# The order of reads in a paged-attention kernel: queries before probabilities, and the second query weights one slot sooner

## The chip, the cores and the metric

The kernel runs on one core of a Trainium2 chip, in one launch. The metric is the time of the execution on the device in microseconds (us). Single executions of the same kernel differ: the three timed ones of the kernel before lie between 1224.23 and 1229.9 us.

## The reference: what is computed

Everything is float32. There are B = 8 sequences of S = 128 tokens with 512 channels. First each sequence gets a LoRA-like product with the adapter that its id selects, and then attention over a paged cache and over its own new keys and values:

```
x = x + einsum('bsi,boi->bso', x, weight[adapter_ids])          # 512 x 512 per sequence
q, k, v = x @ Wq.T, x @ Wk.T, x @ Wv.T                          # 32 query heads, 8 key heads, D = 128
q, k = rope(rmsnorm(q, q_norm_w), pos), rope(rmsnorm(k, k_norm_w), pos)
k_all = concat([k_cache[block_table], k]);  v_all = concat([v_cache[block_table], v])   # 512 + 128 keys
scores = q . k_all / sqrt(128), cache keys past cache_seqlens masked out
o = softmax(scores) . v_all                                     # 4 query heads share a key head
x = x + o @ Wo.T
```

## The kernel before, in words

**Groups and steps.** The 8 key heads are cut into G = 4 groups of 2, each with its 8 query heads. The main loop runs over 32 steps: step i is group g = i // 8 and sequence b = i % 8. The weights of a group are loaded once and serve its 8 steps; steps 7, 15 and 23 are the last of their groups and already project the first sequence of the next group.

**Slots.** A step has 8 slots, h = 0 to 7, one for each query head of the group; slot number 8 * i + h orders them all. Heads 0 to 3 are the first half (j = 0), heads 4 to 7 the second (j = 1). In a slot TensorE computes the scores sc of one head (line 977, 128 queries by 640 keys) from the turned queries qT and the turned keys kT; VectorE adds the mask and takes the row's extreme (line 987); ScalarE takes the exponential (line 1003); GpSimd multiplies by the reciprocal of the row's sum (line 1052). Between the scores TensorE does pieces of a list called main: projections pj_kv and pj_q for step i + 1, products of probabilities and values o for step i - 1, and the output projection out for step i - 2 or i - 1. All these pieces are issued at line 508. From step 6 on main holds, in this order, pj_kv and q0's pj_q of step i + 1, o of step i - 1 for the first half, q1's pj_q of step i + 1, o of step i - 1 for the second half, and out. In steps 1 to 5 o comes first and the adapter's product y is among them.

**Turning by way of DRAM.** Operands that TensorE needs turned (transposed) are turned in blocks of 32 by VectorE, written to DRAM, and read back in another order. There are four such streams, named by their tiles:

- probabilities of one half: tp is written to xp (send, line 837, 1280 KB), and xp is read to pT (receive, line 846, 1280 KB);
- queries of one half: tq to xq (send_q, line 757, 256 KB), xq to qT (line 764, 256 KB);
- keys of a step: tk to xk (line 739, 512 KB), xk to kT per key head (line 747, 256 KB);
- weights of the next group, in pieces of 128 rows: tw to xw (line 465, on ScalarE's queue), and xw to w_kv, w_q or w_o (receive_weights, line 473, 256 KB each, on ScalarE's queue). In the profile q0 and q1, the weights of the first and of the second four query heads, both show as w_q. Each has four pieces, n = 0 to 3, and a projection needs all four.

**Who issues what.** Writes and reads of probabilities, queries and keys are issued by SyncE (SP) in program order; reads of turned weights by ScalarE (ACT), between its computations; the gathers of cached keys and values kc and vc by GpSimd. A read waits for the landing of the write that it follows. The framework gives every transfer of SP and ACT one of eight semaphores, which are used again and again, and an issue also waits for the last transfer of its semaphore.

**When a read is issued.** A read of probabilities or queries isn't issued in the slot of its write but in a later one. The list to_read keeps it with its write's slot number; in each slot, after the exponential and the weight reads, those of earlier slots are issued in the order in which they were appended. send(u) appends in the slot after a half's fourth head; a query's send_q is called from the list later, run just after that, so that in a slot where both are appended the probabilities stand first. Reads of weights stand in a table by slot, made before the loop: read_at(slot, key). With B = 8, kv's four reads are in slots h = 2 to 5 of a group's seventh step (6, 14 and 22), q0's in slots 4 to 7 of it, and q1's in its slot 7 and in slots 0 to 2 of the next step. The tile of q1 has one buffer; its old weights are last used by the projection for the group's last sequence, in slot 4 of the seventh step.

Of the kernel before, what the change touches and what calls it, by code (L numbers as in the profile page):

```python
# [19 lines left out]
B = 8  # L20
# [32 lines left out]
def lora_then_paged_attention(  # L53
# [219 lines left out]
    def read_at(slot, key):  # L273
        reads_at.setdefault(slot, []).append(key)

    for g in range(1, G):
        before = 8 * B * (g - 1)
        for k, kind in enumerate(("kv", "q0", "q1")):
            for n in range(4):
                turn_when[before + 9 + 5 * (4 * k + n) // 2] = len(turns_of)  # L280
                turns_of.append((kind, g, n))
                read_at(before + 8 * (B - 2) + (2, 4, 7)[k] + n, (kind, g, n))
        for n, slot in enumerate((39, 42, 45, 62, 64, 66, 68, 70)):
            key = (f"o{n // 4}", g, n % 4)
            turn_when[before + slot] = len(turns_of)
            turns_of.append(key)
            read_at(8 * (B * g + 1) + n - n // 4 * 2, key)
# [440 lines left out]
    to_read = []  # L728
# [23 lines left out]
    def send_q(i, n):  # L752
        s = st[i]
        tq = work.tile([P, 4, 4, Q4], FP, tag=f"tq{n}", name=f"tq_{i}_{n}")
        nc.vector.transpose(tq, s.q[n].rearrange("p h (a d) -> p a h d", a=4))
        xq = xch.tile([4, P, 4, Q4], FP, tag=f"xq{n}", name=f"xq_{i}_{n}")
        nc.sync.dma_start(
            out=xq.rearrange("b (i a) h q -> (b i) (a h q)", a=4),
            in_=tq.rearrange("p a h q -> p (a h q)"),
        )  # L760

        def receive():
            s.qT[n] = work.tile([P, 4, 4, Q4], FP, tag=f"qT{n}", name=f"qT_{i}_{n}")
            nc.sync.dma_start(
                out=s.qT[n].rearrange("d b h q -> d b (h q)"),
                in_=xq.rearrange("b d h q -> d b (h q)"),
            )

        to_read.append((now[0], receive))

    now = [0]

# [69 lines left out]
    def receive(u):  # L842

        pl, tag = (lora, "raw") if u.j and u.i >= B - 3 else (pts, "pT")
        pT = pl.tile([P, 4, REP, QK], FP, tag=tag, name=f"pT_{u.i}_{u.j}")
        nc.sync.dma_start(
            out=pT.rearrange("p b r k -> p b (r k)"), in_=u.scr.rearrange("b p x -> p b x")
        )
        st[u.i].pT[u.j] = pT

    def run(queue):
        calls = list(queue)
        queue.clear()
        for f in calls:
            f()
# [80 lines left out]
    for i, (g, b) in enumerate(steps):  # L936
        s = st[i]
        main = []
        if i == 0:
            main += project(0, "q1")  # L940
        early = i >= B - 2
        if i and not early:
            main += values(i - 1, 0)
        if i < last:
            main += project(i + 1, "kv") + project(i + 1, "q0")
        if early:
            main += values(i - 1, 0)
        if i == last:
            main += output(i - 2)
        if g == 0 and b + 2 < B and i:  # L950
            main += lora_y(b + 2)
        if i and not early:
            main += values(i - 1, 1)
        if i < last:
            main += project(i + 1, "q1")
        if early and i < last:
            main += values(i - 1, 1)
        if i == 0:
            main += lora_y(2)
        if i == last:  # L960
            pieces = output(i - 1)
            main += pieces[:3] + values(i - 1, 1, True) + pieces[3:]
        elif i and i != last - 1:
            main += output(i - 1)
        unit = None
        for h in range(8):
            j, r = h // 4, h % 4
            if r == 0:
                unit = Unit()
                unit.i, unit.j, unit.p = i, j, {}  # L970
                unit.mn, unit.sm, unit.rc = (
                    small.tile([P, REP], FP, tag=t, name=f"{t}_{i}_{j}") for t in ("mn", "sm", "rc")
                )

            sc = ps_sc.tile([P, 1024], FP, tag="sc", name=f"sc_{i}_{h}")
            for lo, hi in ((0, L), (L, LA)):
                nc.tensor.matmul(  # L977
                    sc[:, lo:hi],
                    lhsT=s.qT[j][:, r, :, :].rearrange("d h q -> d (h q)"),
                    rhs=s.kT[j].rearrange("d a c i -> d (a c i)")[:, lo:hi],  # L980
                    start=True,
                    stop=True,
                )
            p = probs.tile([P, LA], FP, tag="p", name=f"p_{i}_{h}")
            unit.p[r] = p
            one = slice(r, r + 1)
            nc.vector.tensor_tensor_reduce(  # L987
                out=p,
                in0=sc[:, 0:LA],
                in1=masks[i % 2].rearrange("p a c i -> p (a c i)"),  # L990
                scale=1.0,
                scalar=3.0e38,
                op0=ALU.add,
                op1=ALU.min,
                accum_out=unit.mn[:, one],
            )
            now[0] = 8 * i + h
            run(pending)
            turns = turns_at.pop((i, h), [])
            for early, _, f in turns:  # L1000
                if early:
                    f()
            nc.scalar.activation(  # L1003
                p, p, AF.Exp, bias=unit.mn[:, one], scale=-1.0, accum_out=unit.sm[:, one]
            )
            if prev is not None:
                u, pr = prev
                if u.i < last or u.j == 0:
                    turn_p(u, pr)
                if pr == REP - 1:  # L1010
                    send(u)
                    to_read.append((8 * i + h, lambda u=u: receive(u)))
            run(later)
            run(to_write)
            if 8 * i + h in turn_when:
                to_write.append(send_weights(*turns_of[turn_when[8 * i + h]]))
            for key in reads_at.get(8 * i + h, []):
                receive_weights(*key)
            for _ in range(len(to_read)):
                when, f = to_read.pop(0)  # L1020
                if when < 8 * i + h:
                    f()
                else:
                    to_read.append((when, f))
            if h == 0 and i:
                receive_k(i, 1)
            if h == (1 if i else 3) and i < last:
                send_k(i + 1)
            if h == 4 and i < last:
                receive_k(i + 1, 0)  # L1030

            ahead = sum(c for k in range(h + 1, 8) for _, c, _ in turns_at.get((i, k), []))
            mine = sum(t[1] for t in turns)
            share = (sum(c for c, _ in main) + ahead + mine) / (8 - h) - mine
            took = 0.0
            while main and (h == 7 or took + main[0][0] / 2 <= share):
                cost, f = main.pop(0)
                f()
                took += cost
            for early, _, f in turns:  # L1040
                if not early:
                    f()
            if i == last and h > 4:
                turn_p_pe(*prev)
            nc.vector.reciprocal(unit.rc[:, one], unit.sm[:, one])  # L1045
            q = p
            if i == last and j == 1:

                unit.p[r] = probs.tile([P, LA], FP, tag="p", name=f"pk_{h}")
                p = p.rearrange("q (a c i) -> q a c i", a=4, c=NC)  # L1050
                q = unit.p[r].rearrange("q (c i a) -> q a c i", a=4, c=NC)
            nc.gpsimd.tensor_scalar(q, p, unit.rc[:, one], 1.0, ALU.mult, ALU.mult)  # L1052
            prev = (unit, r)

            if i < last:
                if i + 1 < last and h in ((3, 5) if i else (4, 5)):
                    c = 0 if h < 5 else 2
                    gather_k(i + 2, c)
                    gather_k(i + 2, c + 1)
                for c in {6: (0, 1), 7: (2, 3)}.get(h, ()) if i else (range(LC) if h == 7 else ()):  # L1060
                    gather_v(i + 1, c)
                if h == 6:
                    pending.append(lambda i=i: make_mask(i + 1))
            if g == 0 and h == 6 and b + 3 < B:
                load_x(b + 3)
                gather_lora(b + 3)
            if 8 * i + h - 1 in turn_when:
                load_next()
# [58 lines left out]
```

## Time and profile before

| what | value |
|---|---|
| median of three runs | 1227.44 us (1224.23 to 1229.9) |
| the profiled execution's own time | 1228.89 us |
| its span, first to last instruction | 1227.1 us |
| mean granted TensorE clock | 0.99 |
| TensorE (PE) busy | 1188.1 us, 97% |
| VectorE (DVE), GpSimd (POOL), ScalarE (ACT) busy | 729.9, 675.3 and 531.0 us |
| bytes moved by DMA | 328.26 MB, 267 GB/s over the span |

The page and the answers of the trace name an engine, a line and the tiles: `PE sc L977 <- DMA qT<-xq` is TensorE's work on the scores at line 977, which waited for the transfer from xq to qT. Matmuls overlap and their ends are modelled, so the start of one is the safer mark. A line of a timeline gives start and length in us, the engine, the line, the operation and the tiles, how many were merged (x), and in brackets the idle time before and who ended it. SPq and ACTq are the issuing of DMAs; the length there is that of the issue, not of the transfer. The time to landing comes from a query on the single transfer. Steps are told from each other by the first score matmul of each: step 6 starts at 289.96 us, step 7 at 330.18, step 15 at 612.07 and step 23 at 896.60.

### The profile page before, as it was taken

To read this page: it belongs to the slowest core of one execution; us is meant where nothing else is said; L and a number is where in the kernel's file an instruction comes from. 1 tells how busy PE (TensorE), PEld (TensorE's weight loads), DVE (VectorE), ACT (ScalarE), POOL (GpSimd) and SP (SyncE) were. 2 spreads that over 40 slices of the span, in tenths; PEclk is the share of its full clock that TensorE was granted. 3 is DMA by queue.
4 is the path that set the end of the run, shared out by engine and by line. 5 is a ranking of instruction groups with operands and counts; after the bars stand their busy time and mean duration, and the time that the engine had idled before them with its cause. 6 is when DMAs were issued, how large, how long until landed. Compare 5 with 4: busy or idle time off the path is not lost.

```text
span 1227.1 us, 12945 instructions
## 1 busy us (share of the span) xinstructions
PE 1188.1 (97%) x3408; PEld 579.5 (47%) x3408; DVE 729.9 (59%) x1670; ACT 531.0 (43%) x1649; POOL 675.3 (55%) x778
## 2 busy tenths in 40 slices
PE   5889999999899999999989999999989999999998
PEld 3554554454344444444434444444434444444445
DVE  4456666565466666666547666666556656655651
ACT  4454444444344444444434444444434444444442
POOL 5464546455555556556635556655555566555541
PEclk9989999999899999999989999999999999999999
DMA  8267798877878989888878998888898897777761
GB/s 298 87 233 246 257 310 276 282 252 264 266 253 282 334 293 323 279 297 275 294 244 278 311 353 285 286 296 283 275 297 264 281 306 244 263 232 256 260 226 60
DMA packets 187496, 328.26 MB, mean 267 GB/s; under 512 B 13440, under 2 KB 106496, under 8 KB 178336
## 3 DMA queue, kind: packets, MB, share of 16 engines
q1 hardware_dynamic: 124112, 239.23, 58.1%
q10 hardware_dynamic: 50096, 48.22, 12.1%
q0 software_dynamic: 13216, 39.99, 9.7%
q8 instruction: 27, 0.44, 0.1%
q14 instruction: 45, 0.37, 0.1%
HBM read 195.27 MB, written 132.12 MB: 267 GB/s over the span
## 4 chain that ended last, share of the span: by engine, by line
PE 91%; DMA 3%; POOL 2%; ACT 2%; issue 1%; DVE 1%; ACTq 0%
PE sc L977 22%; PE o L508 21%; PE pj_q L508 18%; PE out L508 17%; PE pj_kv L508 9%; PE y L508 2%; DMA qT<-xq 1%; PE lw L430 1%; DMA bt_i<-in_itok_Bx_dram 1%; DMA w_q<-xw_q 1%; DMA xq<-tq 1%; DMA w_o<-xw_o 1%; PE x L430 1%; PE kt L711 1%; ACT sq L595 0%
## 5 line engine op out<-in xcount | busy, mean ns | idle before, releaser
L987 DVE CUSTOM_DVE_ANT_0 p<-sc,mask 128x640 f32<-128x640 f32 x256 | 211.0, 824 | 425.0 <-PE sc L977 424.8
L1003 ACT ACTIVATE p<-p,mn 128x640 f32<-128x640 f32 x256 | 211.6, 827 | 346.8 <-DVE mn L987 337.2
L977 PE MATMUL sc<-kT,qT 128*128 128x512 f32 (+1 forms) x1024 | 320.9, 436 | 7.8 <-DMA qT<-xq 4.1
L1052 POOL TENSOR_SCALAR p<-p,rc 128x640 f32<-128x640 f32 x252 | 201.6, 800 | 211.8 <-DVE rc L1045 210.0
L977 PEld LDWEIGHTS sc<-kT,qT 128*128 128x128 f32 x1024 | 191.0, 191 | 235.5 <-issue 213.4
L508 PE MATMUL pj_q<-w_q,x1T 128*128 128x512 f32 x512 | 242.6, 605 | 8.5 <-DMA w_q<-xw_q 4.0
L508 PE MATMUL o<-pT,vc 128*128 128x512 f32 x512 | 237.4, 594 | 0.0
L508 PE MATMUL out<-w_o,oT 128*128 128x512 f32 (+1 forms) x528 | 235.1, 580 | 2.1 <-ACT oT L786 0.7
L819 DVE STREAM_TRANSPOSE tp<-p 128x640 f32<-128x640 f32 x252 | 211.0, 837 | 4.4 <-POOL p L1052 4.1
L559 POOL DMA_INDIRECT kc<-in_L_cond_k_cache_dram,key_ix x128 | 130.9, 1023 | 31.8 <-issue 30.2
L559 POOL DMA_INDIRECT vc<-in_L_cond_v_cache_dram,val_ix x128 | 128.2, 1002 | 31.2 <-issue 31.2
L508 PEld LDWEIGHTS pj_q<-w_q,x1T 128*128 128x128 f32 x512 | 94.1, 195 | 103.6 <-issue 100.5
L640 ACT ACTIVATE q<-q,rs 128x128 f32<-128x128 f32 x256 | 81.9, 391 | 139.1 <-POOL q L627 136.0
L508 PEld LDWEIGHTS out<-w_o,oT 128*128 128x128 f32 x528 | 95.7, 190 | 95.1 <-issue 91.5
L508 PEld LDWEIGHTS o<-pT,vc 128*128 128x128 f32 x512 | 92.2, 191 | 89.0 <-issue 81.8
L508 PE MATMUL pj_kv<-w_kv,x1T 128*128 128x512 f32 x256 | 118.7, 602 | 0.7 <-ACT x1T L432 0.7
L620 POOL TENSOR_TENSOR k<-sw 128x256 f32<-128x256 f32 x31 | 22.9, 740 | 159.8 <-PE kt L711 134.4
L627 POOL TENSOR_TENSOR q<-q,sw 128x512 f32<-128x512 f32 x61 | 77.2, 1265 | 48.6 <-DVE sw L611 48.6
L595 ACT ACTIVATE sq<-pj_q 128x128 f32<-128x128 f32 x256 | 70.7, 276 | 48.3 <-PE pj_q L508 40.3
L635 POOL TENSOR_TENSOR rs<-ss,mhalf 128x6 f32<-128x6 f32 x64 | 77.6, 1213 | 5.3
L508 PEld LDWEIGHTS pj_kv<-w_kv,x1T 128*128 128x128 f32 x256 | 46.8, 194 | 47.4 <-issue 45.7
L508 PE MATMUL o<-pT,vn 128*128 128x512 f32 x128 | 65.4, 593 | 0.0
(112 smaller groups left out, 866.3 us busy)
## 6 DMA issues: line engine op xcount, KB each, us to landing
xp<-tp SPq DMA_DIRECT2D x63, 1280.0 KB, 5.8
pT<-xp SPq DMA_DIRECT2D x63, 1280.0 KB, 6.8
xk<-tk SPq DMA_DIRECT2D x31, 512.0 KB, 7.7
kT<-xk SPq DMA_DIRECT2D x62, 256.0 KB, 6.5
xq<-tq SPq DMA_DIRECT2D x59, 256.0 KB, 4.3
qT<-xq SPq DMA_DIRECT2D x59, 256.0 KB, 6.1
st_q<-in_L_cond_Wq_dram ACTq DMA_DIRECT2D x24, 256.0 KB, 5.4
xw_q<-tw_q ACTq DMA_DIRECT2D x24, 256.0 KB, 4.0
```

The lines of the kernel that those rows point to most:

```text
L430: nc.tensor.transpose(t[:, j, :], blk, ident)
L508: nc.tensor.matmul(y[0], lhsT=lhsT, rhs=rhs, start=(k == 0), stop=(k == len(pieces) - 1))
L559: nc.gpsimd.indirect_dma_start(out=dst[:, c, :], out_offset=None, in_=src, in_offset=bass.IndirectOffsetOnAxis(ap=rows[:, g, at : at + 1], ...
L595: nc.scalar.activation(sq, t[:, h, :], AF.Square, scale=float(D) ** -0.5, accum_out=ss[:, h : h + 1])
L627: nc.gpsimd.tensor_tensor(dst, cw, sw[:, 0:heads, :], ALU.add)
L635: nc.gpsimd.tensor_tensor(rs[:, 0:width], ss[:, 0:width], mhalf[:, 0:width], ALU.pow)
L640: nc.scalar.activation(q, q, AF.Identity, scale=rs[:, h : h + 1])
L819: nc.vector.transpose(u.tp[:, :, r, :], u.p.pop(r).rearrange("q (a k) -> q a k", a=4))
L977: nc.tensor.matmul(sc[:, lo:hi], lhsT=s.qT[j][:, r, :, :].rearrange("d h q -> d (h q)"), rhs=s.kT[j].rearrange("d a c i -> d (a c i)")[:, ...
L987: nc.vector.tensor_tensor_reduce(out=p, in0=sc[:, 0:LA], in1=masks[i % 2].rearrange("p a c i -> p (a c i)"), scale=1.0, scalar=3.0e38, op0 ...
L1003: nc.scalar.activation(p, p, AF.Exp, bias=unit.mn[:, one], scale=-1.0, accum_out=unit.sm[:, one])
L1052: nc.gpsimd.tensor_scalar(q, p, unit.rc[:, one], 1.0, ALU.mult, ALU.mult)
```

## The change

Two things. An entry of to_read gets a rank, 0 for queries and 1 for probabilities, and the entries that are due in a slot are issued in the order of rank. And the four q1 reads of each group are put into the table one slot sooner: slots 6 and 7 of the group's seventh step and slots 0 and 1 of the next.

```diff
         for k, kind in enumerate(("kv", "q0", "q1")):
             for n in range(4):
                 turn_when[before + 9 + 5 * (4 * k + n) // 2] = len(turns_of)
                 turns_of.append((kind, g, n))
-                read_at(before + 8 * (B - 2) + (2, 4, 7)[k] + n, (kind, g, n))
+                read_at(before + 8 * (B - 2) + (2, 4, 6)[k] + n, (kind, g, n))
...
-        to_read.append((now[0], receive))
+        to_read.append((now[0], 0, receive))
...
                 if pr == REP - 1:
                     send(u)
-                    to_read.append((8 * i + h, lambda u=u: receive(u)))
+                    to_read.append((8 * i + h, 1, lambda u=u: receive(u)))
...
             for key in reads_at.get(8 * i + h, []):
                 receive_weights(*key)
-            for _ in range(len(to_read)):
-                when, f = to_read.pop(0)
-                if when < 8 * i + h:
-                    f()
-                else:
-                    to_read.append((when, f))
+            due = [r for r in to_read if r[0] < 8 * i + h]
+            to_read[:] = [r for r in to_read if r[0] == 8 * i + h]
+
+            for _, _, f in sorted(due, key=lambda r: r[1]):
+                f()
             if h == 0 and i:
                 receive_k(i, 1)
```

## The prediction

> **What bounds the kernel now.** I read the page's busy times first.
>
> ```profile
> PE 1188.1 (97%) x3408; PEld 579.5 (47%) x3408; DVE 729.9 (59%) x1670; ACT 531.0 (43%) x1649; POOL 675.3 (55%) x778
> ```
>
> TensorE is busy for 1188.1 of 1227.1 us and the next engine for 730. Only TensorE's 39 us of idle time, and whatever slows its clock, can be won by moving transfers. So the second view is the waits of TensorE alone: who released it, sum, times, longest.
>
> ```profile
> PE lw L430 <- DMA raw_lora<-in_L_cond_weight_dram: 7.7, 1, 7.7
> PE sc L977 <- DMA qT<-xq: 4.1, 1, 4.1
> PE pj_q L508 <- DMA w_q<-xw_q: 4.0, 1, 4.0
> PE pj_q L508 <- issue: 3.9, 1, 3.9
> ```
>
> The first is the start of the program. The other three are single waits of about 4 us. The timeline of TensorE puts them at 326.13-330.18, 627.82-631.78 and 912.35-916.23: the three changes of group, in steps 7, 15 and 23. The third has no named releaser, but the last read of w_q before it, issued at 907.88, took 8.2 us and landed at 916.04, so it is the same wait as the second.
>
> ```profile
> 626.80 1.02 PE L508 MATMUL o<-pT,vn 128*128 128x512 f32 x2
> 631.78 5.28 PE L508 MATMUL pj_q<-w_q,x1T 128*128 128x512 f32 x6 [3.96 <-DMA w_q<-xw_q]
> 636.90 1.24 PE L977 MATMUL sc<-kT,qT 128*128 128x512 f32 x4
> ```
>
> Six such matmuls take 2.74 us elsewhere and 5.28 after this wait. The stages say the same (columns: window, length, busy per engine, granted clock, DMA share, GB/s): the step of the wait, the undisturbed step after it, and the wait's own surroundings.
>
> ```profile
> 612.07:653.35 41.28, 37.32 (x95) 17.26 (x94) 21.19 (x50) 15.16 (x49) 20.27 (x24) 0.92 0.80 260
> 653.35:688.00 34.65, 34.65 (x96) 16.42 (x95) 24.02 (x53) 15.18 (x49) 20.46 (x24) 1.00 0.89 296
> 627.80:637.00 9.20, 5.24 (x8) 2.28 (x8) 1.82 (x7) 1.82 (x5) 2.85 (x4) 0.63 0.52 183
> ```
>
> The clock is 0.63 around the wait. A step without a wait repeats at 34.62 us from first score matmul to first score matmul, so a wait of 3.96 us costs 41.28 - 34.62 = 6.66.
>
> Two queue timelines show what is late. SP's at the first change of group:
>
> ```profile
> 311.54 0.33 SPq L837 DMA_DIRECT2D xp<-tp  x1
> 312.14 0.32 SPq L757 DMA_DIRECT2D xq<-tq  x1
> 318.56 0.37 SPq L846 DMA_DIRECT2D pT<-xp  x1
> 319.59 0.36 SPq L764 DMA_DIRECT2D qT<-xq  x1
> ```
>
> The 1280 KB read pT goes 1.0 us ahead of the 256 KB read qT. pT took 8.9 us and landed at 327.5; qT took 10.5 and landed at 330.05, 2.5 us behind it. ACT's at the second:
>
> ```profile
> 609.71 1.07 ACTq L473 DMA_DIRECT2D w_q<-xw_q  x2
> 614.33 0.37 ACTq L473 DMA_DIRECT2D w_q<-xw_q  x1
> 618.84 0.37 ACTq L473 DMA_DIRECT2D w_q<-xw_q  x1
> 623.36 0.43 ACTq L473 DMA_DIRECT2D w_q<-xw_q  x1
> ```
>
> The pair at 609.71 is the fourth q0 read and the first q1 read; the others are q1 reads two to four, one per slot. The last took 8.2 us, in company with a pT read, and landed at 631.54. The third took 6.0 and landed at 624.9.
>
> [...] waits of 3.9 to 4.05 us are followed by matmuls at up to double time (four score matmuls in 2.48 instead of 1.24 us at 330.18). The 0.65 us wait at 434.79 (step 9) made its step 35.51, a cost of 0.89: nearly its own length. [...]
>
> **The change part by part.** The built programs differ by no instruction on PE, DVE or POOL. On SP six pairs of reads swap: qT of step i goes ahead of pT of step i-1 for second halves in steps 2 to 6, and qT_7_0 goes ahead of pT_6_0. On ACT twelve reads (four q1 pieces, three times) move up one slot. Nothing is added.
>
> *Swap at step 7.* qT still waits for xq until 319.57, so its issue hardly moves; it loses pT in front. kT, the transfer before it, landed at 320.4. One 256 KB read takes about 2.5 us (330.05 - 327.5), so qT lands near 323-324, ahead of the 326.13 at which TensorE wants it. The wait of 4.05 goes. The slow stretch behind it goes too: the next score started 7.66 us later (330.18 to 337.84) where 4.52 is regular, so 3.14. Sum 7.19.
>
> *q1 reads at step 7.* The fourth was issued at 344.61, took 4.9 and landed at 349.5; TensorE waited until 349.71 (0.63, put down to ACT in the waits, though that was done). The interval was 5.38 against 4.51: 0.87. One slot earlier it is in time. Sum 0.87.
>
> *q1 reads at steps 15 and 23.* The fourth now goes out in the third's place: 618.84 and 903.37, landing (6.0 and 5.8) near 624.9 and 909.2, against 627.8 and 912.35. Spare: 2.9 and 3.2. Gains: 41.28 - 34.62 = 6.66, and 40.43 (896.60 to 937.03) - 34.62 = 5.81.
>
> *Swaps at steps 2 to 6.* No TensorE wait stands there, so they gain nothing here. pT is issued 1.2 us later (SP 136.29 and 137.09: the gap and one issue) and behind qT's bytes, and xk, queued next, moves as little. pT used to land at 145.4 and qT at 146.5; swapped, pT takes the later place. It is first used at 149.95: 3.4 spare. At step 6 it would land by 308, used at 311.44. Cost zero while that lasts; without it, each us missed costs at least one, six times.
>
> *What the first q1 read does.* It now leaves in the slot of q0's third read and stands ahead of q0's fourth in ACT's row. At step 15 q0's fourth landed at 616.9 and the next read 0.85 later, at 617.75; q0's projection starts at 617.66. Swapped places make it 0.1 + 0.24 (from landing to matmul, 631.54 to 631.78) = 0.3 late. At step 23 it would land at 901.85 for 902.19: just in time. At step 7 the projection moves to 338.92 - 7.19 = 331.7, and q0's fourth landed at 331.6; one read later would cost 0.9 + 0.2, but q0's third read (issued 319.83, landed 329.6) no longer stands wholly behind pT, so I take 0.4. With the 0.65 -> 0.89 ratio, together 0.9; bounds 0 and 3. On ACT it also stands ahead of the kT copy, which has 4 us (607.75 to 612.07). Each issue reuses one of eight semaphores and waits for that one's last transfer: at step 7 the first q1 read for a w_q read landed at 319.7, just before; ACT idles 9.1 us soon after.
>
> *Next late.* The pT read of the second half: at 623.41 (landed about 630.4), needed at 638.84 - 6.66 = 632.2, and no longer sharing with a q1 read. At step 23: 914.1 against 922.52 - 5.81 = 916.7. At step 7 SP holds xp until qT_7_1 is out at 331, so pT lands near 344 (xp 5.5, pT 7.0) against 346.2. Spare 1.8 to 2.6: no cost taken, 0 to 2 in the range.
>
> Sum: 7.19 + 0.87 + 6.66 + 5.81 - 0.9 = 19.6. The profiled execution took 1228.89 itself (span 1227.1), 1.45 above the median 1227.44: 1209.3 from it, 1207.8 from the median. I take **1208.5**.
>
> **Rivals.** (1) q0's fourth read becomes the late one: the tight margins above speak for it, the 0.85 us spacing of landings against more than 0.5. At 2 us each with some slow clock, three times 3: 1218. (2) The swap at step 7 does not help, because all transfers there share the engines and qT's 10.5 us is their load; for it, xq itself took 7.4; against it, qT landed right after pT. Then 7.2 less: 1216. (3) Slower: SP's queue. In steps 2 to 7 pT, xk and the next writes now stand behind qT's wait for xq. If that pushes pT past its 3.4 us at each of six places, [...] as priced above at 6.7. It decides once pT lands more than 7.4 us later than now; six such, 40, beat the 20 gained: 1248. The traced gap of 0.8 to 1.1 us between the two issues speaks against it. (4) The change does nothing that counts: another transfer, pT of the second half, stops TensorE at the same places within 6 us: 1222.
>
> **How the numbers follow.** About 0.5% (6.1 us) is what a measurement of this kernel can tell from no change. Chances: my forecast 0.67, (1) 0.14, (2) 0.11, (4) 0.05, (3) 0.03. Faster 0.92, same 0.05, slower 0.03. The range: forecast bounds run from 1228.89 - 20.5 - 1.45 - 1.9 = 1205 (no new cost, a little more where qT's spare of 0.4 to 0.6 us in steps 2 to 6 was used up in other executions) to 1213 (costs 3 and 2); taking in (2) makes it 1217.
>
> **What would show it.** Right: TensorE's waits lose all three 4 us rows; steps 15 and 23 last 34.6 to 35.2 us; the clock stays near 1.00 there; qT at step 7 lands within 5 us. Wrong in part: a wait at pj_q two slots before the old one (rival 1), at sc in step 7 (rival 2), at o from pT in steps 2 to 7 (rival 3) or right behind the removed waits (rival 4).

## The result, and the profile after

| kernel | median of its runs, us | lowest to highest |
|---|---|---|
| before | 1225.84 | 1222.3 to 1229.9 |
| after | 1210.08 | 1207.79 to 1210.96 |

The ratio of after to before is 0.9868, with a 95% interval of 0.9831 to 0.9904: faster by 1.3%. The forecast was 1208.5 (1205 to 1217). The profiled execution of after took 1210.85 us, with a span of 1209.1 and a mean clock of 0.997. It is 18.04 us shorter than the profiled one of before; the sum of the prediction was 19.6.

The page's busy times come first, as before. TensorE has lost 7.8 us of busy time, though it issues the same 3408 matmuls. That is slow clock that is gone (0.50 for 6.83, 6.83 and 3.41 us behind the three waits before): what the matmuls took there beyond their regular time comes to 3.3, 2.7 and 1.9 us.

```profile
PE 1180.3 (98%) x3408; PEld 577.2 (48%) x3408; DVE 729.9 (60%) x1670; ACT 531.0 (44%) x1649; POOL 675.2 (56%) x778
```

TensorE's waits (who released it, sum, times, longest):

```profile
PE lw L430 <- DMA raw_lora<-in_L_cond_weight_dram: 7.4, 1, 7.4
...
PE out L508 <- ACT p L1003: 2.0, 1, 2.0
...
PE out L508 <- DMA w_o<-xw_o: 1.3, 1, 1.3
...
PE pj_q L508 <- issue: 0.5, 1, 0.5
PE o L508 <- DMA pT<-xp: 0.2, 1, 0.2
```

The three rows of about 4 us are gone. What is left near their places is 0.5 us at pj_q in step 7, for q0's weights. Two rows at out are new in size: they stand in steps 9 and 17, the second step of the second and of the third group, and were 0.65 and 0.64 us before.

The timeline of TensorE at the second change of group. The six matmuls of q1 that took 5.28 us behind a wait take 2.74, with no wait in brackets:

```profile
621.35 2.74 PE L508 MATMUL pj_q<-w_q,x1T 128*128 128x512 f32 x6
623.92 1.24 PE L977 MATMUL sc<-kT,qT 128*128 128x512 f32 x4
```

The stages (window, length, busy per engine in the order PE, PEld, DVE, ACT, POOL, granted clock, DMA share, GB/s) say the same: step 15, the step behind it, and the 9.2 us around the former wait.

```profile
605.60:640.38 34.78, 34.78 (x96) 16.48 (x95) 21.18 (x50) 15.17 (x49) 20.25 (x24) 1.00 0.95 308
640.38:675.03 34.65, 34.65 (x96) 16.43 (x95) 24.02 (x53) 15.18 (x49) 20.45 (x24) 1.00 0.89 294
620.40:629.60 9.20, 9.20 (x28) 4.42 (x27) 4.37 (x11) 4.83 (x17) 5.71 (x8) 1.00 0.84 305
```

Step 15 is as long as its neighbour but for 0.13 us, and the clock, 0.63 around the wait before, is 1.00.

SP's queue at the first change of group, and ACT's at the second:

```profile
311.28 0.33 SPq L837 DMA_DIRECT2D xp<-tp  x1
311.87 0.32 SPq L757 DMA_DIRECT2D xq<-tq  x1
...
319.30 0.37 SPq L764 DMA_DIRECT2D qT<-xq  x1
319.76 0.48 SPq L846 DMA_DIRECT2D pT<-xp  x1
```

```profile
603.24 2.18 ACTq L473 DMA_DIRECT2D w_q<-xw_q  x2
...
607.85 0.37 ACTq L473 DMA_DIRECT2D w_q<-xw_q  x1
...
612.37 0.37 ACTq L473 DMA_DIRECT2D w_q<-xw_q  x1
```

On SP the two have changed places, and qT landed at 323.62, 4.3 us after its issue instead of 10.5. On ACT the last read of q1 now leaves at 612.37, ahead of the pT read at 617.87 instead of beside one, and landed at 619.30.

Step lengths, first score matmul to first score matmul, add up to the difference of the profiled executions. Step 6 is 36.00 and the others are 34.62 where none of these waits stands.

| place | before | after | measured | in the forecast's sum |
|---|---|---|---|---|
| steps 6 and 7 | 78.86 | 71.32 | -7.54 | -7.7 (7.19 + 0.87 - 0.4) |
| step 9 | 35.51 | 36.83 | +1.32 | 0 |
| step 15 | 41.28 | 34.78 | -6.50 | -6.4 (6.66 - 0.3) |
| step 17 | 35.50 | 36.13 | +0.63 | 0 |
| step 23 | 40.44 | 34.62 | -5.82 | -5.8 |
| sum | | | -17.91 | -19.6 (the 0.4 and 0.3 entered it as 0.9) |

Both kernels were profiled a second time (below). The same five places then took 231.22 us before and 212.83 after, so 18.4 less.

### The profile page after: what moved, and what is told of

Same layout as the page of the kernel before. It is cut to its first block, busy times and chain, and to the rows that moved or that the text cites. A ratio compares the mean times of both kernels' runs of the same rounds, so it can differ in the third digit from the quotient of the medians.

```text
span 1209.1 us, 12947 instructions
## 1 busy us (share of the span) xinstructions
PE 1180.3 (98%) x3408; PEld 577.2 (48%) x3408; DVE 729.9 (60%) x1670; ACT 531.0 (44%) x1649; POOL 675.2 (56%) x778
## 4 chain that ended last, share of the span: by engine, by line
PE 93%; DMA 2%; ACT 1%; POOL 1%; DVE 1%; issue 1%; ACTq 0%; SPq 0%
PE sc L977 22%; PE o L508 22%; PE out L508 18%; PE pj_q L508 18%; PE pj_kv L508 9%; PE y L508 2%; PE lw L430 1%; DMA bt_i<-in_itok_Bx_dram 1%; DMA w_o<-xw_o 1%; PE x L430 1%; PE kt L711 1%; DMA pT<-xp 0%; DMA xp<-tp 0%; ACT sq L595 0%; DVE p L987 0%
## 5 line engine op out<-in xcount | busy, mean ns | idle before, releaser
L508 PE MATMUL pj_q<-w_q,x1T 128*128 128x512 f32 x512 | 238.1, 595 | 0.5 <-issue 0.5
```

Of the source, the lines that this page charges most:

```text
L508: nc.tensor.matmul(y[0], lhsT=lhsT, rhs=rhs, start=(k == 0), stop=(k == len(pieces) - 1))
```

## The experiments

All ratios are to the kernel before, in runs on the same chip. Three sets were run: the first with before at 1228.19 us (median of 33 runs, 1220.08 to 1231.74), the second at 1227.08, the third at 1225.61. The ratios are those on record with their intervals; they need not be the quotient of two medians. A step's "extra" below is its length less the undisturbed length and less the wait itself.

### The swap alone

```diff
-read_at(before + 8 * (B - 2) + (2, 4, 6)[k] + n, (kind, g, n))    # after
+read_at(before + 8 * (B - 2) + (2, 4, 7)[k] + n, (kind, g, n))    # as in before
```

> The swap alone (queries read ahead of probabilities; q1's reads where they were). My theory: the wait at the first scores of step 7 goes (4.05 us and 3.14 of slow clock), q1's fourth read stays late in steps 7, 15 and 23, so about 7.2 us less than the kernel before, near 1219, steps 15 and 23 at 41.3 and 40.4 us. Rival (shared load, not order, made qT late): no more than 1 us less, near 1225, with a wait of 3 to 4 us at sc in step 7. On the output weights: if the wait at out in step 9 grew from 0.65 to 1.97 us because step 7 lost its stall, it is near 2 here in step 9 and near 0.65 in step 17; if it is chance, neither need hold.

Measured: 1224.65 us (1221.05 to 1231.63), ratio 0.9998 [0.9974, 1.0021]. The swap alone gains nothing that can be told: by the interval at most 0.26%, about 3 us. The forecast of 7 us less was a miss. The time is the rival's, but its wait of 3 to 4 us at sc is not there. The waits show why:

```profile
PE pj_q L508 <- issue: 8.6, 2, 4.6
...
PE pj_q L508 <- ACT p L1003: 1.4, 1, 1.4
```

The wait at sc is gone, as intended. One of the two waits of the first row is new, and it is in the same step 7, at the start of q1's projection:

```profile
345.48 4.34 PE L508 MATMUL pj_q<-w_q,x1T 128*128 128x512 f32 x6 [4.61 <-issue]
```

Steps 6 and 7 together took 76.99 instead of 78.86. The wait had moved by 15 us, and was not gone: before, TensorE had stood still for 4 us ahead of q1's projection, and so found q1's fourth read late by only 0.63 us. The second execution below has the landings that settle how.

### The swap alone, once more, and before once more

> The swap alone a second time, for the size of its waits. If the wait for the second query weights at step 15, 1.39 us in the first execution, is a matter of chance, it comes out anywhere between 1.4 and 4.5 now, while those at steps 7 and 23 stay at 4 to 5; the time is 1221 to 1231. If 1.39 belongs to the order of the reads, it is 1.4 again within 0.3.

Measured: 1228.52 us. Waits 4.03 (step 7), 4.04 (step 15), 4.16 (step 23); steps 6 and 7 together 76.59. The 1.39 at step 15 did not come back, so it was chance and not the order of the reads. The landings: SP issued pT of the second half at 337.73, and ACT q1's fourth read half a microsecond later:

```profile
337.73 0.36 SPq L846 DMA_DIRECT2D pT<-xp  x1
```

```profile
338.22 0.40 ACTq L473 DMA_DIRECT2D w_q<-xw_q  x1
```

This read took 8.3 us and landed at 346.52; the matmul followed at 346.71. In before, the same pair left at 340.46 and 344.61, 4.15 us apart, and the read took 4.9. So the stall for qT had not only given the read more time, it had also set it behind most of the pT transfer. Without the stall it runs beside all of it.

> The kernel before a second time, as a yardstick. The three waits at steps 7 (scores), 15 and 23 (second query weights) are there again; that at step 15 lies between 1.4 and 4.5 if chance moves it by the amount seen in the swap alone, at 3.96 within 0.3 if not. The time is 1220 to 1232.

Measured: 1228.91 us. Waits 4.17 at step 15 and 4.24 at step 23, and in step 7 2.47 at sc and 2.04 at q1 instead of 4.05 and 0.63. The two waits of step 7 trade against each other between executions of one kernel: their sum, 4.51 and 4.68, hardly moves.

### The q1 reads alone

```diff
-        to_read.append((now[0], 0, receive))    # after; the order of to_read as in before
+        to_read.append((now[0], receive))
```

> The earlier q1 reads alone (probabilities still ahead of queries). My theory: steps 15 and 23 fall to 34.6 to 35 us, so about 12.3 less than before, plus 0.9 in step 7; near 1213; the wait of about 4 us at the first scores of step 7 stays. The rival in which q0's fourth read takes over: a wait of 2 us or more at q0's projection in steps 15 and 23, and 1217 or more. On the output weights: if the lost stalls cause it, the wait at out is near 1.3 in step 17 and near 0.65 in step 9.

Measured: 1214.12 us (1213.13 to 1216.91), ratio 0.9901 [0.9869, 0.9932]. Steps 15 and 23 fell to 34.85 and 34.62. The wait for the queries stayed, and steps 6 and 7 together took 75.98:

```profile
PE sc L977 <- DMA qT<-xq: 3.7, 1, 3.7
```

So at the first change of group the swap alone gives 1.87 (2.27 in its second execution), the reads alone 2.88, and both 7.54. Each part removes a wait behind which the other one hides. The sum of two lone trials would have been 4.75. These gains are counted from before's first execution. In its second the two steps took 77.30, and from there they are 0.31 to 0.71, 1.32 and 5.98: the sizes move with chance by 1.6 us, but both together bring far more than the sum each time.

### The q1 reads one slot sooner still

```diff
-(2, 4, 6)[k] + n
+(2, 4, 5)[k] + n
```

> The changed kernel with q1's reads yet one slot sooner (slots 5, 6, 7 of the group's seventh step and 0 of the next), so that two of them, not one, stand ahead of q0's fourth read in ScalarE's queue. My theory of places in the queue: q0's fourth lands some 0.9 to 1.2 us later than in the changed kernel, so the waits at q0's projection grow to about 1.4 us in step 7, 1.1 in step 15 and 0.9 in step 23, in all 3 us more than the changed kernel, near 1213. Rival (the order within the queue does not matter, the transfers share the engines): the waits stay at 0.5 us and less, and the time is that of the changed kernel, 1210.

Measured: 1212.39 us (1210.92 to 1213.37), ratio 0.9888 [0.984, 0.9935]. Waits for q0's fourth read: 1.50 at step 7, 0.82 at step 15, 0.77 at step 23 (after: 0.46 at step 7, under 0.2 at the other two; in its second execution 0.41, 0.79 and under 0.2).

```profile
333.49 3.67 PE L508 MATMUL pj_q<-w_q,x1T 128*128 128x512 f32 x8 [1.50 <-issue]
```

The place in ACT's queue counted here, as the prediction's first rival said: by the lengths of the steps, two reads ahead of q0's fourth instead of one cost 1.1 us more at step 7 and 0.8 to 1.0 at step 23, but at step 15 0.9 or 0.1, depending on which execution of after is compared. The loss in time, about 2 us between the medians, lies within the intervals. Sooner than the slot that was needed was no better here.

### The q1 reads two slots later than in after

```diff
-(2, 4, 6)[k] + n
+(2, 4, 8)[k] + n
```

> The changed kernel with q1's reads one slot later than in the kernel before (slots 0 to 3 of the next step), the swap kept. My theory: the fourth read goes out 4.5 us later than before, so TensorE waits 8 to 8.5 us in steps 15 and 23 and 4.5 to 5.5 in step 7; the slow stretch after the wait does not grow with it (1.8 to 2.7 us, as after 3.9), so steps 15 and 23 last 45 to 46 us and the time is near 1219 + 14 = 1233. Rival (the slow clock costs in proportion to the wait): 5 us of slow stretch at each, near 1240.

Measured: 1230.34 us (1228.14 to 1232.5), ratio 1.0023 [1.0011, 1.0035].

```profile
PE pj_q L508 <- DMA xq<-tq: 15.0, 3, 5.1
```

The profile puts these waits down to a write of xq. It does the same for the wait at step 15 in before's second execution, where q1's fourth read landed 0.25 us ahead of the matmul and that xq 0.4 us behind its start, so the xq can't be what it waited for. The waits here stand at the same projection: 5.11 us at step 7, where 4.5 to 5.5 was expected, and 4.97 and 4.94 at steps 15 and 23, where 8 to 8.5 was. At these two the fourth read left 4.5 us later in its step than in before, and the wait grew by only 1 us. The later read travelled for less time: at step 15 it left at 627.60 and the matmul began at 632.52, so at most 4.9 us against the 8.2 of the one that left beside a pT read in before (623.36 and 623.41). So I put the old wait of 4 us down to company as well as to lateness. The steps took 41.66, 42.43 and 41.23. Their extras, 1.9, 2.8 and 1.7, are no larger than behind the waits of 3.9 to 4.0 in before (2.7 and 1.9). That speaks against a slow clock in proportion to the wait, but the waits came out only a quarter longer; the last section shows what the extras follow.

### The q1 reads spread, and the o1 reads sooner

After was run again with these: 1209.61 us (1207.93 to 1213.3), ratio 0.9848 [0.9802, 0.9895].

> The changed kernel once more, as a yardstick on the chip of the next three. 1210; waits at out in steps 9 and 17 of 1.3 to 2 us if they belong to the changed kernel, anywhere between 0 and 2 if they are chance.

Its waits were 0.41 at step 7 and 0.79 at step 15 for q0's fourth read, and at out 0.28 in step 9 and 1.04 in step 17. So the 1.97 in step 9 of the first profile is not a fixed price of the change.

```diff
-(2, 4, 6)[k] + n
+((2, 3, 4, 5), (4, 5, 6, 7), (7, 8, 8, 9))[k][n]
```

> The changed kernel with q1's four reads in slots 7, 0, 0 and 1, so that none stands ahead of q0's fourth and the last still goes out in slot 1 of the next step. My theory: q0's waits of 0.46 us in step 7 and 0.16 in step 15 go, and q1's fourth, which now follows the third in slot 1 or 0, is still in time (spare of 2 us or more): 0.6 to 0.9 us less than the changed kernel, near 1209. Rival: q0's fourth was late by load and not by place; nothing changes, or a wait at q1's projection comes back.

Measured: 1209.3 us (1206.56 to 1210.75), ratio 0.9839 [0.9793, 0.9885]. No q1 read stands ahead of q0's fourth, and no wait for q0 or q1 is left in TensorE's list. The time is that of after within the noise: the 0.4 to 0.8 us waits for q0 are too small for the median.

```diff
-            read_at(8 * (B * g + 1) + n - n // 4 * 2, key)
+            read_at(8 * (B * g + 1) + n - n // 4 * 3, key)
```

> The changed kernel with the four reads of the second output weights (o1) one slot sooner, in slots 1 to 4 instead of 2 to 5 of a group's second step. My theory: the wait at out in steps 9 and 17 is for the last of them; read 4.5 us sooner it is in time, the steps fall from 36.8 and 36.1 us to 34.6 to 35, and the time to about 1207. Rival: the wait is for the first output weights or the row's exponential, as the profile names it; then it stays, 1210.

Measured: 1206.8 us (1206.34 to 1208.78), ratio 0.9828 [0.9783, 0.9874]. The four o1 reads (w_o's second half) leave one slot sooner, and the waits at out in steps 9 and 17 are gone; so they were for w_o, though the profile had put one of them down to ACT.

> The changed kernel with both: q1's reads in slots 7, 0, 0 and 1, and o1's one slot sooner. If the two are independent the savings add: 3.5 to 4.5 us less than the changed kernel, near 1206, with no wait of TensorE over 0.5 us between step 1 and step 30 but the 0.67 at step 6. Rival: the transfers moved forward collide with others (o1's reads with step 9's probabilities), and a wait at o from pT takes the place.

Both edits: 1207.23 us (1204.71 to 1208.55), ratio 0.9825 [0.9779, 0.987]. In its profile every step from 7 to 29 takes 34.62 us: no transfer of weights, queries or probabilities stops TensorE at a change of group any more. A wait of 0.99 us for an adapter's read (lraw) stands in step 3, which the expectation did not have, and the savings of the two edits do not add up in the medians. The last two kernels are the lowest measured. Their intervals overlap with that of after, so their gain of 2 to 3 us is likely, not shown; that the waits at out are gone is shown.

### Probabilities one slot later

```diff
-            due = [r for r in to_read if r[0] < 8 * i + h]
-            to_read[:] = [r for r in to_read if r[0] == 8 * i + h]
+            due = [r for r in to_read if r[0] + r[1] < 8 * i + h]
+            to_read[:] = [r for r in to_read if r[0] + r[1] >= 8 * i + h]
```

> The kernel after with every read of probabilities (pT) issued one slot, about 4.5 us, later than its rank would have it; queries keep their place. It prices the margin on which the prediction's third and fourth rivals rest. Theory: a pT read lands as much later as it is issued. The first halves have 8 to 12 us of spare from step 6 on and lose nothing. The second halves have 1.3 to 5.7 us (about 3 in the middle), so some 22 of them become late by 4.5 less their spare, together about 38 us; [...] about 1253 us, with waits at o from pT in almost every step and a clock near 1. Rival: as with the second query weights' fourth read two slots later, the later read meets less company and lands only about 1 us later: then only the places with a spare under 1.5 us show a wait, and the time is 1210 to 1215.

Measured: 1217.69 us (1214.08 to 1227.07), ratio 0.995 [0.9925, 0.9975]. Both theories missed. SP's queue in step 9, first after, then this kernel:

```profile
416.71 0.32 SPq L837 DMA_DIRECT2D xp<-tp  x1
419.57 0.37 SPq L764 DMA_DIRECT2D qT<-xq  x1
420.03 1.43 SPq L747 DMA_DIRECT2D kT<-xk  x1
424.72 0.36 SPq L846 DMA_DIRECT2D pT<-xp  x1
```

```profile
422.04 0.33 SPq L837 DMA_DIRECT2D xp<-tp  x1
424.22 0.37 SPq L764 DMA_DIRECT2D qT<-xq  x1
424.68 1.35 SPq L747 DMA_DIRECT2D kT<-xk  x1
430.81 0.33 SPq L757 DMA_DIRECT2D xq<-tq  x1
431.23 0.39 SPq L846 DMA_DIRECT2D pT<-xp  x1
```

In after this pT left at 424.72, when xp had just landed, at 424.65. From step 7 on, all its pT reads with a recorded landing leave 0.02 to 0.09 us after the landing of their write. So a slot in SP's program was a place in its order here and no time. One slot later puts a first half behind a write of xq, and from step 7 on it left up to 4.1 us after the landing of its write (3.4 in the middle); a second half mostly still left as soon as xp had landed (under 0.1 us in the middle, at most 0.9). The second halves are the tight ones, so TensorE waited 0.2 us in one place for pT, as in after, not 38 us. In its profiled execution, 4.1 us longer than that of after, a wait of 4.13 stands in step 3 for the input of step 4 (acc), whose read left right behind a pT that was itself late. In after the read of acc had little to spare already: it landed at 168.56, 0.6 us before the matmul that waits here.

```profile
172.18 1.09 PE L430 MATMUL x<-ident,acc 128*128 128x128 f32 x4 [4.13 <-DMA acc<-in_x_dram]
```

That step took 47.38 us instead of 40.69. One profile shows this; the median is 7 to 8 us above that of after, and the rest of that stays open.

## Why the prediction was right

**The bound and the three waits.** Right: TensorE's waits were the only stock to win from, the three went, and the clock stayed at 1.00 where it had been 0.63.

**The swap at step 7.** The sum for steps 6 and 7 was right, 7.54 against 7.7; but that is counted from the execution that the sum was read from, and before's second would make it 5.98, so the closeness is luck. Its split was wrong. "Sum 7.19" for the swap and "Sum 0.87" for q1 are not what the parts bring: 1.9 to 2.3 and 2.9 alone, from the same execution. The step that was wrong is the pricing of q1 at step 7 by the 0.63 us wait in before (0.87 with what follows it). That wait was measured behind a 4 us stall, which covered the same read. The landing of qT was right: "near 323-324", measured 323.62.

**q1 at steps 15 and 23.** Right: 6.66 and 5.81 predicted, 6.50 and 5.82 measured. But the landing was foretold by the wrong neighbour. I gave the fourth read the third's 6.0 and 5.8 us; it took 6.9 and 6.5. Why is not shown; at step 15 the read ahead of it was still under way for 1.46 us, against 0.49 for the third in before. Spare of 2.9 and 3.2 covered that.

**q0's fourth read.** Predicted 0.4, 0.3 and about 0 at steps 7, 15 and 23; measured by step length beyond the undisturbed 0.70, 0.16 and 0.00: 0.86 together against 0.9. After's second execution had 0.41 and 0.79 at steps 7 and 15. With two reads ahead the waits were 1.50, 0.82 and 0.77, and with none they vanished, so the place ahead of q0's fourth is what made it late; how late varied: at step 15 it cost after 0.16 us in one execution and 1.03 in the other.

**Swaps at steps 2 to 6.** Right at zero. The second halves' pT left 1.3 to 1.7 us after the landing of its write where the landings are recorded, 0.1 before; 1.2 had been taken. In step 2 it landed at 145.82 with 3.86 us of spare, in step 6 at 307.49 with 3.69. Rival 3 needed 7.4 us, an estimate of mine from 3.4 of spare and a stall as long as those of before, about 4. The kernel with pT one slot later speaks against it too: even there no wait for pT over 0.2 us arose. What it did cost came by acc, a road that no rival had named.

**Next late.** pT of the second half kept 1.97, 1.31 and 1.80 us of spare, where 2.2, 1.8 and 2.6 were predicted. No wait came of it.

**The term that was missing.** Steps 9 and 17 took 1.95 us more than in before, by waits at out of 1.97 and 1.27 for the last w_o read. The sum of 19.6 had no such term, and 1.95 is more than its whole error of 1.6. It is partly chance: in step 9 the wait was 0.28 to 1.97 over the executions, in step 17 0.32 to 1.34. In step 17 it was 1.0 to 1.3 in after and the swap alone, twice each, and in the spread q1 reads; it was 0.3 to 0.8 in before, twice, in the q1 reads alone and with q1 sooner and later, though the reads and writes of SP and ACT are issued in the same order there in all of these. That the lost stalls make these waits grow did not hold: the swap alone, which loses one in step 7, had 0.54 in step 9, and the q1 reads alone, which lose one in step 15, had 0.32 in step 17. Why is open.

## What to carry to other kernels

Price two late transfers in one stage together: the second one's wait in the trace is only what is left of it behind the first, so each edit alone may bring less than its share of what both bring (1.87 and 2.88 us alone, 7.54 together at the first change of group). Ask of a late read not only when it is issued but what runs beside it; set in front of a large transfer it may gain more than its shift (q1's fourth read at step 15 left 4.5 us sooner in its step and landed 5.8 us sooner); set beside it, it may lose (8.3 us on its way instead of 4.9, in the swap alone at step 7). And a slot in the program of SP, which only issues transfers, gave an order here and not a time (after's pT reads left 0.02 to 0.09 us after the landing of their write): look for the landing that the issue really waits for.

## What the runs showed of the hardware that was not expected

**What a wait cost beyond its length.** Waits up to 2.04 us made their step longer by the wait and 0.19 to 0.27, whether short or long (0.33 by 0.57, 1.39 by 1.63, 1.97 by 2.21). So in these waits the addition hardly changed with their length; the prediction had taken it for a ratio. Whether it is a real cost of starting again or lies in how the trace reads a gap, no run shows. Waits of 3.7 to 5.1 us cost 1.7 to 3.3 on top, with no trend in their length (4.61: 1.8; 4.94: 1.7; 3.99: 3.2). And the second execution of before has slow matmuls after a shorter wait:

```profile
329.23 1.99 PE L977 MATMUL sc<-kT,qT 128*128 128x512 f32 x4 [2.47 <-DMA qT<-xq]
```

The four score matmuls take 1.24 us elsewhere. The next score started 6.28 us after this one instead of 4.51: 1.77 on top of a wait of 2.47, while its wait of 2.04 at q1 cost 0.23 on top.

The granted clock in the traces goes with this. In before it changes at 329.55, 336.38, 629.92, 636.75, 916.64 and 920.06 us, which lie 2, 86, 2, 82 and 1 times 3.413 us apart; in after, at 62.76, 66.17, 83.23 and 86.65 us, 1, 5 and 1 times as far. The slow stretches behind the waits, at a clock of 0.50, lasted one or two times 3.413 us. Of the stalls after step 1 over all traces, the nine with one of them had extras of 1.7 to 1.9 us, the seven with two 2.6 to 3.3. Here are two stretches of 3.41 us at each of the two waits in before's second execution, the one where TensorE idled most and the one behind it (columns as in the first section: behind the window and its length stands TensorE's busy time, and third from the end the clock):

```profile
326.32:329.73 3.41, 0.94 (x3) 0.30 (x2) 0.00 (x0) 0.00 (x0) 1.99 (x3) 1.00 1.13 345
329.73:333.14 3.41, 3.41 (x7) 1.77 (x6) 1.89 (x4) 0.92 (x2) 0.00 (x0) 0.50 0.87 243
...
346.79:350.20 3.41, 1.42 (x4) 0.73 (x5) 1.75 (x5) 1.74 (x5) 1.40 (x2) 1.00 0.33 119
350.20:353.62 3.42, 3.42 (x11) 1.69 (x10) 0.91 (x3) 0.04 (x1) 1.45 (x2) 1.00 0.27 86
```

TensorE idled for 2.47 us of the first, and the next ran at 0.50; it idled for 1.99 of the third, and the clock stayed at 1.00. Cut in the same way, from one change of the clock to the next by 3.413 us, before and after have seven stretches at full clock between 25 and 1150 us with 2.00 us or more of idle time, four of them before 84 us, and each was followed by one at 0.50; no other had more than 1.27, and none of those was. Where a wait stood against such a stretch differed between executions, so part of its price was chance. What sets the clock, no run here shows.

**A small read beside a large one.** q1's fourth read (256 KB) took 8.2 to 8.5 us in the seven recorded places where it left within 0.5 us of a pT read (1280 KB) of the other queue. It took 6.3 us where it left 3.43 us behind the pT read, and 4.9 at 4.15 us. In all nine a write of keys (xk, 512 KB) follows the pT read on SP's queue, so the company is both. These are not prices for every small read: in after, q0's third read left 0.19 us ahead of a pT read at 319.57 and took 4.9, and 0.31 us behind one at 599.47 and took 9.6. How the bytes were shared, no run here measured.
